# A kernel of conditioned attention: VectorE's last addition of K's first and of K's second products is made in two halves

## The chip, the cores and the metric

The kernel runs on one core of one Trainium2 chip. The metric is the device time of one execution in microseconds (us), given as the median of several runs. TensorE, VectorE, ScalarE, GpSimd and SyncE are the core's engines; in the profile's rows they are PE (its weight loads PEld), DVE, ACT, POOL and SP.

## What is computed

For each of 8 batch elements x has 512 rows of 512 numbers, and the heads are 16 of 32 numbers each. All is fp32. Cut to what matters, the reference is:

```python
Q = split_heads(x @ Wq.T + bq)          # 8 x 16 x 512 x 32; K and V likewise
tQ = split_heads(tokens @ Wq.T + bq)    # one conditioning row per batch element; tK likewise
cQ, cK = Q + tQ, K + tK
scores = einsum('bhqd,bhkd->bhqk', cQ, cK) / sqrt(32)
out = einsum('bhqk,bhkd->bhqd', softmax(scores), V)
return x + out.transpose(0, 2, 1, 3).reshape(8, 512, 512)
```

## The kernel before

**Tiling.** The heads are taken four at a time: four heads of 32 numbers fill the 128 partitions, so a batch element has G = 4 groups of heads, and there are T = 32 groups, numbered t. For a group, TensorE makes the scores with queries in the partitions (`row_scores`, L641), VectorE takes their row maxima (L593, L650), ScalarE makes exponentials of half of them with their row sums (L701). The other half is made with keys in the partitions (`exponentials_of_rest`, `joined`: L772 puts the maxima into PSUM, L785 adds the scores, L799 takes the exponential). VectorE and DMAs turn the kept half (L660, L682), and TensorE multiplies by V (L840). PSUM is one tile of 8 banks of 512 columns that the code hands out itself: `banks(i)` is the i-th bank of the current order, `released` says in which order banks come free, and the next step's scores go into them.

**Projections by seven products.** Q, K and V of the next batch element are made between these steps. For two groups at a time (u = 0 or 1) the 2 x 2 blocks of weights and x are combined so that seven products of half size do (`product`, L462; each is eight matmuls of 256 columns, four for half of it). They come in two parts. *First* makes products 1, 7, 6 and half of product 2; *other*, called second here, makes 4, 5, the other half of 2, and 3. The four results of a pair of groups are c1 (128 x 512, as two halves of 256), c2 (likewise), and c12 and c22, which are the right halves of c1 and c2. For K, c1 and c2 are the two groups' K as later scores read it.

- K's first (`first_by_others` with `mixed` None): products 1 and 7 fill one bank (`one_`), 6 and then 2 another (`two_`; 6 its right half, 2 its left). VectorE copies the first bank to c2 (L530) and sets c1 to the second bank plus the copied product 1 on both halves (L531). GpSimd then adds c12 to c22 (L533).
- K's second (`other_products` with `bias`): products 4 and 5 fill one bank, 2 and then 3 another (2 the left half, 3 the right). VectorE adds to c12 (L555), makes c2 with its bias (L557, recorded as L487 in `plus`), and adds the second bank and the bias to c1 (L560, recorded as L487).

**The order of the work** is written out by hand: `thirds(t, made)` holds, for each of the 28 groups t = 1 to 28, three steps (i = 0, 1, 2), each with scores, exponentials and one of the twelve items of the list `MADE`. One group out of two has K's first as its last item; K's second is the second item of the following group. The projections of batch elements 1 to 7 are made there, so each of the two stands 14 times. Each engine executes its own instructions in the order in which they are written. An instruction waits on semaphores of other engines, and of its own, where it needs their results or their room.

Of the kernel before, what the change touches and what calls it, by code (L numbers as in the profile page):

```python
# [12 lines left out]
ALU = mybir.AluOpType  # L13
# [4 lines left out]
def kernel(  # L18
# [38 lines left out]
    nc = tc.nc  # L57
# [58 lines left out]
    def banks(i, n=1):  # L116

        row = row_of[0] or [at_end[j] for j in TURNS[turn[0]]]
        j = row[i]
        if n == 1:  # L120
            return psum[:, j, :]
        k = row[i + 1]
        return psum[:, j : k + 1 : k - j, :]
# [273 lines left out]
    def pair_of(t, n):  # L397

        if (n, t // 2) not in pairs:
            pairs[n, t // 2] = qkp.tile([P, 2, S], F32, tag=n, name=f"{n}T_{t // 2}")  # L400
        return pairs[n, t // 2]
# [50 lines left out]
    def product(n, b, u, i, pt, kcs=(0, 1)):  # L452

        for kc in kcs:
            w = block_of_w(n, i, u, kc)
            if n == "v":
                still, moving = block_of_x(b, i, kc, slice(u * P, (u + 1) * P)), w
            else:
                still, moving = w, block_of_x(b, i, kc, slice(0, HS))
            for j in range(HG):  # L460
                r = slice(j * HD, (j + 1) * HD)
                nc.tensor.matmul(  # L462
                    pt[r], still[:, r], moving, start=(kc == kcs[0]), stop=(kc == kcs[-1])
                )

    def twice(a):
        return a.unsqueeze(1).broadcast_to([P, 2, HS])

    def halves(a):
        return a.rearrange("p (h s) -> p h s", h=2)  # L470


    def parts_of(n, b, u):

        if n == "v":
            v = vs[b % 2]
            return v[:, u::2, :HS], v[:, u + 2, :HS], v[:, u::2, HS:], v[:, u + 2, HS:]
        o = pair_of(b * G + u * 2, n)
        return halves(o[:, 0, :]), o[:, 0, HS:], halves(o[:, 1, :]), o[:, 1, HS:]

    def plus(n, b, u, g, o, pt, rest):

        if n == "v":
            nc.vector.tensor_tensor(o, pt, rest, ALU.add)
        else:
            add = tok[:, "qk".index(n), u * 2 + g, b : b + 1]
            nc.vector.scalar_tensor_tensor(o, pt, add, rest, ALU.add, ALU.add)  # L487
# [22 lines left out]
    def first_by_others(n, b, u, dens, at, last, mixed):  # L510

        one_, two_ = halves(banks(at[0])), halves(banks(at[1]))
        c1, c12, c2, c22 = parts_of(n, b, u)
        product(n, b, u, 1, one_[:, 0])
        product(n, b, u, 7, one_[:, 1])
        product(n, b, u, 6, two_[:, 1])
        product(n, b, u, 2, two_[:, 0], (0,))
        if mixed:
            dens((0, 1))
            nc.scalar.copy(c2, one_)  # L520
            dens((2, 3))
            nc.vector.tensor_tensor(c1, two_, twice(c2[:, 0, :]), ALU.add)
            last()
        else:
            dens((0, 1))
            if mixed is False:
                dens((2, 3))
            if mixed is None:
                dens((2, 3))
                nc.vector.tensor_copy(c2, one_)  # L530
                nc.vector.tensor_tensor(c1, two_, twice(c2[:, 0, :]), ALU.add)  # L531
                last()
                nc.gpsimd.tensor_tensor(c22, c22, c12, ALU.add)  # L533
                return
            else:
                nc.scalar.copy(c2, one_)
                nc.scalar.copy(c1, two_)
            last()
            nc.gpsimd.tensor_tensor(c12, c12, c2[:, 0, :], ALU.add)
            nc.gpsimd.tensor_tensor(c22, c22, c12, ALU.add)  # L540
            nc.gpsimd.tensor_tensor(c1[:, 0, :], c1[:, 0, :], c2[:, 0, :], ALU.add)
            return
        nc.gpsimd.tensor_tensor(c22, c22, c12, ALU.add)

    def other_products(n, b, u, dens, small, at, bias=False):

        dens()
        one_, two_ = banks(at[0]), banks(at[1])
        product(n, b, u, 4, one_[:, :HS])
        product(n, b, u, 5, one_[:, HS:])  # L550
        small()
        product(n, b, u, 2, two_[:, :HS], (1,))
        product(n, b, u, 3, two_[:, HS:])
        c1, c12, c2, c22 = parts_of(n, b, u)
        nc.vector.tensor_tensor(c12, one_[:, HS:], c12, ALU.add)  # L555
        if bias and n != "v":
            plus(n, b, u, 1, c2, halves(one_), twice(c22))  # L557
        else:
            nc.vector.tensor_tensor(c2, halves(one_), twice(c22), ALU.add)
        plus(n, b, u, 0, c1, halves(two_), c1)  # L560
        if n != "v":
            for g in range(2):
                qkT[n, b * G + u * 2 + g] = pair_of(b * G + u * 2, n)[:, g, :]
# [462 lines left out]
    advance()  # L1026
    row_max(0, 2)
    other_products("q", 0, 1, lambda: denominators(0, 2), nothing, (0, 1))
    advance()
    row_max(0, 3)  # L1030
# [5 lines left out]
    row_max(1, 0)  # L1036
    transpose_max(0, banks(1), nc.scalar.copy)
    other_products("k", 0, 1, lambda: denominators(1, 0), nothing, (0, 2))
    turn_x(NC + 1)
    load_blocks()  # L1040
# [44 lines left out]
    row_max(1, 2)  # L1085
    denominators(1, 2)
    other_products("v", 0, 0, nothing, nothing, (0, 2))
    turn_x(NC + 3)
    load_blocks()
# [32 lines left out]
    def products(b, n, u, product, alone, dens, last, plain):  # L1122

        if product == "first":
            first_by_others(n, b, u, dens, (4, 5) if alone else (0, 1), last, plain)
        else:
            at = (4, 5) if alone else (0, 3)
            if n == "v" and not plain:
                other_by_others(n, b, u, dens, nothing, at)
            else:  # L1130
                other_products(n, b, u, dens, nothing, at, True)
            last()
        if alone:
            released(6, 7, 0, 1, 2, 3, 4, 5)
        elif product == "first":
            released(2, 3, 4, 5, 6, 7, 0, 1)
        else:
            released(1, 2, 4, 5, 6, 7, 0, 3)
# [118 lines left out]
    def one_item(b, n, u, product, at, dens, last):  # L1257

        if n == "v" and product == "first":
            first_of_v(b, u, at)  # L1260
        elif product == "first":
            first_by_others(n, b, u, dens, at, last, False)
        elif n == "v":
            other_by_others(n, b, u, dens, nothing, at)
        else:
            other_products(n, b, u, dens, nothing, at, True)
# [182 lines left out]
    b, g = divmod(t, G)  # L1449
# [52 lines left out]
```

## Time and profile before

| what | value |
| --- | --- |
| median of 3 runs | 649.97 us (649.82 to 650.51) |
| span of the profiled execution | 648.4 us |
| time of the profiled execution by itself | not recorded apart from the three runs; their median lies 1.6 us above the span |
| mean granted TensorE clock | 0.998 |
| busy: PE, DVE, ACT, POOL | 641.6, 600.1, 533.9, 410.6 us |
| VectorE instructions | 845 |

A row of the timeline gives the start in us from the start of the span, the duration in us, engine, line, operation, tile written and tiles read, shape, how many equal instructions were merged, and in brackets how long the engine was idle before it and what ended that. A row of the groups gives count, busy time, mean ns of one, and idle time before. A row of the waits says who waited for whom: us in total, times, longest. The starts of neighbouring rows of an engine can lie closer than a duration, since an operation's end overlaps the next one's beginning. TensorE's matmul ends are modelled.

### The profile page before, as it was taken

To read this page: it belongs to the slowest core of one execution; us is meant where nothing else is said; L and a number is where in the kernel's file an instruction comes from. 1 tells how busy PE (TensorE), PEld (TensorE's weight loads), DVE (VectorE), ACT (ScalarE), POOL (GpSimd) and SP (SyncE) were. 2 spreads that over 40 slices of the span, in tenths; PEclk is the share of its full clock that TensorE was granted. 3 is DMA by queue.
4 is the path that set the end of the run, shared out by engine and by line. 5 is a ranking of instruction groups with operands and counts; after the bars stand their busy time and mean duration, and the time that the engine had idled before them with its cause. 6 is when DMAs were issued, how large, how long until landed. Compare 5 with 4: busy or idle time off the path is not lost. (4 is left out here: it accounts for less than half of the span.)

```text
span 648.4 us, 24814 instructions
## 1 busy us (share of the span) xinstructions
PE 641.6 (99%) x9856; PEld 356.7 (55%) x9856; DVE 600.1 (93%) x845; ACT 533.9 (82%) x1364; POOL 410.6 (63%) x651
## 2 busy tenths in 40 slices
PE   9999999999999999999999999999999999999997
PEld 8445555556555555555555555555555555555531
DVE  3799999999999999999999999999999999999887
ACT  2479888889888989888888988898988888898564
POOL 3633655686665776758567776558766576665650
PEclk9999999999999999999999999999999999999999
DMA  7615688878888788977888978788888767797921
GB/s 191 107 27 84 131 164 172 168 169 191 168 171 174 158 182 177 200 156 153 181 178 170 201 154 186 161 175 169 179 193 162 153 144 164 153 188 155 199 48 34
DMA packets 248457, 102.02 MB, mean 157 GB/s; under 512 B 229962, under 2 KB 230474, under 8 KB 248340
## 3 DMA queue, kind: packets, MB, share of 16 engines
q1 hardware_dynamic: 234196, 65.54, 53.6%
q0 software_dynamic: 12384, 33.83, 20.2%
q8 instruction: 78, 1.28, 0.8%
q10 hardware_dynamic: 1760, 1.05, 0.5%
q14 instruction: 39, 0.32, 0.1%
HBM read 19.75 MB, written 8.39 MB: 43 GB/s over the span
## 5 line engine op out<-in xcount | busy, mean ns | idle before, releaser
L593 DVE TENSOR_REDUCE nmax<-psum 128x1 f32<-128x512 f32 x279 | 177.5, 675 | 9.3 <-PE psum L641 4.9
L701 ACT ACTIVATE psum<-psum,nmax 128x512 f32<-128x512 f32 x248 | 165.3, 678 | 3.6 <-DVE nmax L593 3.0
L641 PE MATMUL psum<-kT,qT 32*128 32x512 f32 x1024 | 162.0, 612 | 0.0
L701 ACT ACTIVATE store<-psum,nmax 128x512 f32<-128x512 f32 x204 | 139.6, 701 | 24.9 <-DVE nmax L593 24.7
L682 POOL DMA_DIRECT2D store<-store x258 | 129.0, 504 | 48.9 <-DMA store<-store 31.8
L799 ACT ACTIVATE store<-psum 128x512 f32<-128x512 f32 x232 | 119.8, 602 | 33.2 <-PE psum L785 33.2
L660 DVE STREAM_TRANSPOSE store<-store 128x1024 f32<-128x1024 f32 x116 | 138.9, 1217 | 0.0
L650 DVE TENSOR_REDUCE nmax<-psum 128x2 f32<-128x1024 f32 x98 | 118.8, 1212 | 0.0
L840 PE MATMUL psum<-store,v 128*32 128x256 f32 x1856 | 106.8, 381 | 0.9 <-DMA store<-store 0.9
L840 PEld LDWEIGHTS psum<-store,v 128*32 128x32 f32 x1856 | 57.2, 110 | 57.9 <-ACT wT_q L632 21.2
L913 POOL TENSOR_TENSOR res<-res,recs 128x512 f32<-128x512 f32 x30 | 31.4, 1046 | 89.0 <-DVE res L912 89.0
L785 PE MATMUL psum<-qT,kT 32*128 32x256 f32 x928 | 83.8, 374 | 0.0
L641 PEld LDWEIGHTS psum<-kT,qT 32*128 32x128 f32 x1024 | 61.5, 183 | 35.4 <-issue 17.8
L785 PEld LDWEIGHTS psum<-qT,kT 32*128 32x128 f32 x928 | 60.8, 184 | 5.9 <-issue 0.3
L701 ACT ACTIVATION_READ_ACCUMULATOR psum<-psum,nmax 128x1 f32 x248 | 55.0, 222 | 0.0
L203 POOL TENSOR_TENSOR xr<-xr,bvs 128x512 f32<-128x512 f32 x30 | 38.6, 1285 | 16.4 <-DMA xr<-in_x_dram 15.7
L462 PE MATMUL psum<-wc_v,xc 128*32 128x256 f32 x768 | 47.7, 379 | 0.0
L462 PE MATMUL psum<-xc,wc_q 128*32 128x256 f32 x720 | 44.7, 379 | 0.0
L462 PE MATMUL psum<-xc,wc_k 128*32 128x256 f32 x720 | 44.5, 379 | 0.0
L701 ACT ACTIVATION_READ_ACCUMULATOR store<-psum,nmax 128x1 f32 x204 | 44.3, 217 | 0.0
L914 POOL TENSOR_TENSOR res<-res,xr 128x512 f32<-128x512 f32 x30 | 38.3, 1278 | 2.3
L462 PE MATMUL psum<-xT,wT_k 128*32 128x256 f32 x480 | 34.5, 382 | 0.0
(191 smaller groups left out, 972.4 us busy)
## 6 DMA issues: line engine op xcount, KB each, us to landing
store<-store SPq DMA_DIRECT2D x264, 128.0 KB, 2.7
store<-store POOLq DMA_DIRECT2D x258, 128.0 KB, 3.8
out_dram<-res SPq DMA_DIRECT2D x122, 64.0 KB, 3.7
xr<-in_x_dram SPq DMA_DIRECT2D x120, 64.0 KB, 4.2
x<-in_x_dram SPq DMA_DIRECT2D x112, 64.0 KB, 3.3
w_q<-in_L_cond_Wq_dram SPq DMA_DIRECT2D x4, 256.0 KB, 3.9
w_v<-in_L_cond_Wv_dram SPq DMA_DIRECT2D x16, 64.0 KB, 2.5
w_k<-in_L_cond_Wk_dram SPq DMA_DIRECT2D x16, 48.0 KB, 2.7
```

Source lines behind the costliest of these rows:

```text
L203: nc.gpsimd.tensor_tensor(xr[t], xr[t], bias, ALU.add)
L462: nc.tensor.matmul(pt[r], still[:, r], moving, start=(kc == kcs[0]), stop=(kc == kcs[-1]))
L593: nc.vector.tensor_reduce(nmax[t][:, qc, j : j + 1, 0], pt, AX.X, ALU.max, negate=True)
L641: nc.tensor.matmul(pt, qkT["q", t][r, qc * P : (qc + 1) * P], qkT["k", t][r, :], start=True, stop=True,)
L650: nc.vector.tensor_reduce(nmax[t][:, qc, pr * 2 : pr * 2 + 2, 0], pt, AX.X, ALU.max, negate=True)
L660: nc.vector.transpose(e, e)
L682: (nc.gpsimd if here else nc.sync).dma_start(to, of)
L701: nc.scalar.activation(to, of, AF.Exp, bias=nmax[t][:, qc, j, :], accum_out=sums[t][:, qc, j, :],)
L785: nc.tensor.matmul(banks(j)[:, i * HS : (i + 1) * HS], qkT["k", t][r, kc * P : (kc + 1) * P], qkT["q", t][r, KQ * P :], start=False, stop= ...
L799: nc.scalar.activation(e[:, j], banks(j), AF.Exp)
L840: nc.tensor.matmul(pt[j * HD : (j + 1) * HD, half * HS : (half + 1) * HS], vs[b % 2][:, kc, (g * HG + j) * HD : (g * HG + j + 1) * HD], e, ...
L914: nc.gpsimd.tensor_tensor(y, y, xr.pop(t), ALU.add)
```

## The change

Both additions that end in c1, at L531 (K's first) and at L560 (K's second), are written as two additions of 256 columns each. In K's first the right half (i = 1, product 6) comes first, in K's second the left half (i = 0, product 2), which is the order in which TensorE issues the products of that bank. Nothing else is changed; line numbers behind L531 move by one, behind L560 by five.

```diff
             if mixed is None:
                 dens((2, 3))
                 nc.vector.tensor_copy(c2, one_)
-                nc.vector.tensor_tensor(c1, two_, twice(c2[:, 0, :]), ALU.add)
+                for i in (1, 0):
+                    nc.vector.tensor_tensor(c1[:, i, :], two_[:, i], c2[:, 0, :], ALU.add)
                 last()
                 nc.gpsimd.tensor_tensor(c22, c22, c12, ALU.add)
                 return
...
-        plus(n, b, u, 0, c1, halves(two_), c1)
+        if bias and n == "k":
+            for i in range(2):
+                plus(n, b, u, 0, c1[:, i, :], halves(two_)[:, i], c1[:, i, :])
+        else:
+            plus(n, b, u, 0, c1, halves(two_), c1)
```

What stands in VectorE's queue at K's first of batch element 1, u = 0, before. The names are those of the built program: kT_1022 is the K of a pair of groups, nmax a group's maxima, and the brackets hold the engines whose semaphores the instruction waits for (PE_49 is TensorE, DVE_49 VectorE itself):

```order
L593 TENSOR_REDUCE nmax_1013<-psum 128x1 [waits PE_49] x2
L650 TENSOR_REDUCE nmax_1013<-psum 128x2 [waits PE_49]
L530 COPY kT_1022<-psum 128x512 [waits PE_49,Activation_49]
L531 TENSOR_TENSOR kT_1022<-psum,kT_1022 128x512 [waits DVE_49,PE_49,Activation_49]
L660 STREAM_TRANSPOSE store<-store 128x4x256
L593 TENSOR_REDUCE nmax_1013<-psum 128x1 [waits PE_49] x3
```

The same place of VectorE's queue in the changed program:

```order
L598 TENSOR_REDUCE nmax_1013<-psum 128x1 [waits PE_49] x2
L655 TENSOR_REDUCE nmax_1013<-psum 128x2 [waits PE_49]
L530 COPY kT_1022<-psum 128x512 [waits PE_49,Activation_49]
L532 TENSOR_TENSOR kT_1022<-psum,kT_1022 128x256 [waits DVE_49,PE_49,Activation_49]
L532 TENSOR_TENSOR kT_1022<-psum,kT_1022 128x256
L665 STREAM_TRANSPOSE store<-store 128x4x256
L598 TENSOR_REDUCE nmax_1013<-psum 128x1 [waits PE_49] x3
```

The one addition became two; the first has all the waits, the second, which reads product 2, has none. K's second of the same pair in VectorE's queue, before:

```order
L650 TENSOR_REDUCE nmax_1013<-psum 128x2 [waits PE_49]
L555 TENSOR_TENSOR kT_1022<-psum,kT_1022 128x256 [waits PE_49,Activation_49,Pool_49]
L487 SCALAR_TENSOR_TENSOR kT_1022<-psum,tok,kT_1022 128x512
L487 SCALAR_TENSOR_TENSOR kT_1022<-psum,tok,kT_1022 128x512 [waits DVE_49,PE_49,Activation_49]
L660 STREAM_TRANSPOSE store<-store 128x4x256
L593 TENSOR_REDUCE nmax_1273<-psum 128x1 [waits PE_49] x2
```

And in the changed program:

```order
L655 TENSOR_REDUCE nmax_1013<-psum 128x2 [waits PE_49]
L556 TENSOR_TENSOR kT_1022<-psum,kT_1022 128x256 [waits PE_49,Activation_49,Pool_49]
L487 SCALAR_TENSOR_TENSOR kT_1022<-psum,tok,kT_1022 128x512 [waits DVE_49]
L487 SCALAR_TENSOR_TENSOR kT_1022<-psum,tok,kT_1022 128x256 [waits PE_49,Activation_49]
L487 SCALAR_TENSOR_TENSOR kT_1022<-psum,tok,kT_1022 128x256 [waits DVE_49]
L665 STREAM_TRANSPOSE store<-store 128x4x256
L598 TENSOR_REDUCE nmax_1275<-psum 128x1 [waits PE_49] x2
```

Here too the wait for TensorE stands at the first half; the second half, which reads product 3, waits for VectorE's own earlier addition to c12. TensorE's queue behind K's second, before; the scores (L641) read this K:

```order
L772 LDWEIGHTS onesb
L772 MATMUL psum<-maxT_957,onesb 128x512 [waits Activation_49]
L785 MATMUL psum<-qT_363,kT_454 128x256 x8
L641 MATMUL psum<-kT_1022,qT_889 128x512 [waits DVE_49,Activation_49]
L641 MATMUL psum<-kT_1022,qT_889 128x512
L641 MATMUL psum<-kT_1022,qT_889 128x512 [waits Activation_49]
L641 MATMUL psum<-kT_1022,qT_889 128x512
L462 MATMUL psum<-wT_v,xc 32x256 [waits Activation_49]
```

TensorE's rows are the same after the change but for their line numbers; the scores then wait for the second half. ScalarE's, GpSimd's and SyncE's rows are the same as well.

## The prediction, made before the changed kernel ran

> **What bounds the kernel now.** I read the page first, for the shares of the engines, then the groups by form for the price of each operation, then the timelines of VectorE, TensorE and the weight loads at one K second and one K first, and last the waits.
>
> ```profile
> PE 641.6 (99%) x9856; PEld 356.7 (55%) x9856; DVE 600.1 (93%) x845; ACT 533.9 (82%) x1364; POOL 410.6 (63%) x651
> ```
>
> TensorE and VectorE are both near full, and neither the 99% nor the 93% says which of them waits for the other. TensorE's rows tell least: the ends of its matmuls are modelled, so its waits show as longer blocks and as idle time of the weight loads (PEld), not as idle time of PE. So I go to the two places of the change. First K's second products, the batch element whose addition starts at 175.41 us; VectorE, TensorE, the weight loads:
>
> ```profile
> 174.16 0.42 DVE L555 TENSOR_TENSOR kT<-psum,kT 128x256 f32<-128x256 f32 x1 [0.18 <-ACT psum L701]
> 174.50 0.74 DVE L487 SCALAR_TENSOR_TENSOR kT<-psum,tok,kT 128x512 f32<-128x512 f32 x1
> 175.41 0.75 DVE L487 SCALAR_TENSOR_TENSOR kT<-psum,tok,kT 128x512 f32<-128x512 f32 x1 [0.17 <-PE psum L462]
> 176.08 1.23 DVE L660 STREAM_TRANSPOSE store<-store 128x1024 f32<-128x1024 f32 x1
> 177.44 1.29 DVE L593 TENSOR_REDUCE nmax<-psum 128x1 f32<-128x512 f32 x2
> ...
> 175.45 1.03 PE L785 MATMUL psum<-qT,kT 32*128 32x256 f32 x16
> 176.31 1.14 PE L641 MATMUL psum<-kT,qT 32*128 32x512 f32 x8
> 177.38 1.07 PE L462 MATMUL psum<-wT_v,xc 128*32 128x256 f32 x16
> ...
> 176.28 0.34 PEld L641 LDWEIGHTS psum<-kT,qT 32*128 32x128 f32 x8 [0.20 <-ACT psum L701]
> ...
> 175.88 0.25 ACT L701 ACTIVATION_READ_ACCUMULATOR psum<-psum,nmax 128x1 f32 x1
> ```
>
> VectorE's last addition (the second L487) waits 0.17 us for TensorE's last product and ends at 175.41 + 0.75 = 176.16. The next scores (L641) read the K that it has just written, and their weight load starts 0.12 us later, at 176.28. The row puts that wait down to ScalarE; but ScalarE's last exponential, with its read-out, had ended at 175.88 + 0.25 = 176.13, so VectorE is the later one. Behind the scores VectorE itself stands idle from 176.08 + 1.23 = 177.31 to 177.44, until they are there. So here the path runs TensorE, this addition, TensorE, VectorE. What the late weights cost TensorE shows beside the same block after q's second products, where the weights were there in time:
>
> ```profile
> 157.65 1.03 PE L641 MATMUL psum<-kT,qT 32*128 32x512 f32 x8
> 158.60 1.07 PE L462 MATMUL psum<-xT,wT_k 128*32 128x256 f32 x16
> ```
>
> There the block takes 158.60 - 157.65 = 0.95 us to the next product, behind K's second 177.38 - 176.31 = 1.07: TensorE already loses 0.12 us here. Now K's first products, the addition at 161.96 us:
>
> ```profile
> 161.04 0.68 DVE L530 COPY kT<-psum 128x512 f32<-128x512 f32 x1
> 161.96 0.69 DVE L531 TENSOR_TENSOR kT<-psum,kT 128x512 f32<-128x512 f32 x1 [0.24 <-ACT store L701]
> 162.56 1.23 DVE L660 STREAM_TRANSPOSE store<-store 128x1024 f32<-128x1024 f32 x1
> ...
> 161.22 0.61 PE L462 MATMUL psum<-xT,wT_k 128*32 128x256 f32 x8
> 161.76 2.07 PE L641 MATMUL psum<-kT,qT 32*128 32x512 f32 x16
> 163.76 2.58 PE L840 MATMUL psum<-store,v 128*32 128x256 f32 x44
> ...
> 162.70 0.30 PEld L641 LDWEIGHTS psum<-kT,qT 32*128 32x128 f32 x7 [0.22 <-DVE kT L531]
> ...
> 164.41 0.69 ACT L701 ACTIVATE store<-psum,nmax 128x512 f32<-128x512 f32 x1 [0.90 <-DVE nmax L593]
> ```
>
> The addition ends at 162.65, and a weight load of the scores, which go into the bank that it read, starts at 162.70: this wait, too, ends at the addition. The block of sixteen lasts 163.76 - 161.76 = 2.00 us to L840; behind V's second products the same sixteen take 1.93:
>
> ```profile
> 104.41 2.00 PE L641 MATMUL psum<-kT,qT 32*128 32x512 f32 x16
> 106.34 3.66 PE L840 MATMUL psum<-store,v 128*32 128x256 f32 x64
> ```
>
> ScalarE cannot take up a delay behind it either: at 164.41 it has waited 0.90 us for VectorE's maxima, which stand behind the addition in VectorE's queue. The waits of the whole run say that these are no single cases:
>
> ```profile
> PEld psum L641 <- DVE kT L531: 2.4, 11, 0.2
> DVE kT L531 <- ACT store L701: 3.4, 14, 0.3
> DVE kT L487 <- PE psum L462: 2.4, 14, 0.2
> ```
>
> **The change part by part.** *What it moves.* It is meant to let VectorE read the half that TensorE finished first while the other half is being made. The rows of the program order (in the section on the change) say that it does not: of the two halves only the first waits for TensorE, and the second, which reads the product that TensorE finishes last, waits for none. Both can be safe only if the first half's wait already stands for the last product. So the first half starts when the whole addition starts now, the 0.17 and 0.24 us of idle time stay, and nothing is removed. TensorE's, ScalarE's, GpSimd's and SyncE's rows are the same before and after. GpSimd's L533 reads only the half written first and may start some 0.3 us sooner; its sum is needed only by K's second, whose first addition (L555) stands at 174.16, some 11 us behind the addition at 162.65, so I count that at nothing; if that cover were gone, it would be a gain of 0.3 us at each. The new waits of VectorE on its own queue are for results at least one operation back that have ended by then: nothing.
>
> On the first half's wait the Trainium skill has a rule, in "PSUM — Partial Sum Buffer", section "PSUM bank collisions raise a hardware error": guard PSUM by bank and quadrant and not by address, since another engine's access to another address of the same bank still collides. Each pair of halves shares one bank, so by that rule the first half has to wait for both products, and the time is the sum below; without it, it is the first rival. The order's rows agree; no timed run here shows it yet.
>
> *What it adds.* Fourteen times (seven batch elements by two halves of the heads) one more VectorE instruction at each of the two places. The price is the distance from start to start, since the end of one operation overlaps the next:
>
> ```profile
> L531 DVE TENSOR_TENSOR kT<-psum,kT 128x512 f32<-128x512 f32 x14 | 9.7, 692 | 3.4 <-ACT store L701 3.4
> L555 DVE TENSOR_TENSOR kT<-psum,kT 128x256 f32<-128x256 f32 x15 | 6.3, 423 | 2.5 <-ACT psum L701 2.3
> L487 DVE SCALAR_TENSOR_TENSOR kT<-psum,tok,kT 128x512 f32<-128x512 f32 x29 | 21.5, 746 | 2.4 <-PE psum L462 2.4
> L487 DVE SCALAR_TENSOR_TENSOR kT<-psum,tok,kT 128x256 f32<-128x256 f32 x1 | 0.5, 483 | 0.1
> ...
> 40.53 0.48 DVE L487 SCALAR_TENSOR_TENSOR kT<-psum,tok,kT 128x256 f32<-128x256 f32 x1
> 40.93 0.70 DVE L372 STREAM_TRANSPOSE xT<-x 128x512 f32<-128x512 f32 x1
> ```
>
> - K's first: a plain addition of 256 columns holds VectorE 174.50 - 174.16 = 0.34 us, two of them 0.68; the one of 512 holds it 162.56 - 161.96 = 0.60. So +0.08 us, fourteen times 1.1 us.
> - K's second: the addition with bias of 256 columns holds it 40.93 - 40.53 = 0.40 us, two of them 0.80; the one of 512 holds it 176.08 - 175.41 = 0.67. So +0.13 us, fourteen times 1.8 us.
>
> The bounds: the trace has no such pair back to back. Below, the second instruction is free if something hides it; a gain is excluded as long as the first half cannot start sooner. Above, with no overlap the durations count: 2 x 0.423 - 0.692 = 0.15 and 2 x 0.483 - 0.746 = 0.22, together 14 x 0.37 = 5.2 us. I take the start-to-start values, since every VectorE row quoted overlaps its successor by about 0.08 us.
>
> The Trainium skill's "Perfetto Trace Analysis", section "Optimizing Scalar/DVE Operations", gives about 125 ns of overhead per VectorE instruction on PSUM; by that, as an estimate, 28 more are 3.5 us, and the time would be 653.5. My rows give 0.08 and 0.13, and they decide.
>
> *What lies on the path.* Both additions end later by what they gain in length, and a TensorE weight load follows each at once (162.70, 176.28). TensorE is already late there by 2.00 - 1.93 = 0.07 and 1.07 - 0.95 = 0.12 us, so no slack is left, and I pass the whole delay on. Between the two places TensorE's blocks stand end to end, and VectorE and ScalarE wait for each other's next step, so I see nothing that gives it back. Sum: 1.1 + 1.8 = 2.9 us. The profiled span becomes 648.4 + 2.9 = 651.3; the median of the runs, 649.97, lies 1.6 us above the span, and with that the time is **652.9 us**.
>
> **The rivals.**
> - *It does what it says (faster).* If the first half waited for its own product alone, K's second could start it at 174.50 + 0.67 = 175.17, the second half at 175.17 + 0.40 = 175.57, and end at 176.05 instead of 176.16: 0.11 us sooner. K's first could start its half when the copy has ended, 161.04 + 0.68 = 161.72, with some 0.04 to the start, and the second 0.34 later at 162.10, ending at 162.52 instead of 162.65: 0.13 sooner. Fourteen times 0.24 is 3.4 us: 646.6. It decides from the point where the idle time before the halves falls under 0.1 us. For it speaks that idle time; against it the single wait in the order's rows. 0.03.
> - *The delay is hidden (same).* Behind q's second, where the weights are in time, an L785 block takes 0.86 us to the scores:
>
> ```profile
> 80.11 1.03 PE L785 MATMUL psum<-qT,kT 32*128 32x256 f32 x16
> 80.97 1.04 PE L641 MATMUL psum<-kT,qT 32*128 32x512 f32 x8
> ...
> 165.50 0.66 DVE L637 TENSOR_REDUCE nmax<-wT_q 128x1 f32<-128x512 f32 x1
> ```
>
>   Behind K's second the scores start at 176.31, which is 175.45 + 0.86, so their first matmul is not late, and VectorE has 0.13 us to spare before 177.44. If the weights may come later still without moving the matmuls, all is covered: 650.0. Against it: the two blocks that are already longer. 0.10.
> - *Only K's second counts (slower).* At K's first the scores held back belong to the second set, which VectorE reads only behind L637 at 165.50, 2.8 us after the weight load; if TensorE makes up those 0.08 us, 1.8 us remain: 651.8. 0.17.
> - *Two halves do not overlap (slower).* 5.2 us: 655.2. 0.06.
>
> **How the numbers follow.** My forecast, both terms on the path, has 0.64. A measurement of this kernel tells about 0.2% (1.3 us) from no change. Slower by more than that: 0.64 + 0.17 + 0.06 = 0.87; within it: 0.10; faster: 0.03. The range 650.8 to 654.0 holds the forecast and the case of K's second alone, 0.81; the hidden case, the faster one and the one without overlap lie outside.
>
> **What would show it.** The idle time before each first half should stay near 0.24 and 0.17 us; the halves should stand 0.34 and 0.40 us from start to start; VectorE's busy time should grow by up to 5.2 us (the durations count there); the weight load behind K's first should wait longer for VectorE than its 2.4 us in all; the blocks behind both should not shrink; the span should be near 651.3. I am wrong in the first step if the idle time before the first halves is gone, and in the last if the additions end later but the next scores' products start at the same distance from L785 as now.

## The result and the profile after

The changed kernel takes **652.42 us** (median of 6 runs, 652.00 to 653.15), the kernel before, timed beside it, 650.25 us (6 runs, 649.82 to 650.83): a ratio of 1.0031, 95% interval 1.0021 to 1.0042. A second timing gave 653.06 against 650.24 us, 1.0039 (1.0026 to 1.0052). So the kernel is slower by 2.2 and 2.8 us, where 2.9 was predicted. The profiled execution of after has a span of 650.2 us at a granted clock of 0.999; before's was 648.4.

The engines' busy times of after, from the page:

```profile
PE 644.1 (99%) x9856; PEld 358.2 (55%) x9856; DVE 601.7 (93%) x873; ACT 533.6 (82%) x1364; POOL 409.8 (63%) x651
```

VectorE has 28 instructions more, and 1.6 us more of busy time, in which overlapping instructions count once. K's first in the timeline of after (VectorE; TensorE; its weight loads):

```profile
161.34 0.68 DVE L530 COPY kT<-psum 128x512 f32<-128x512 f32 x1
162.26 0.76 DVE L532 TENSOR_TENSOR kT<-psum,kT 128x256 f32<-128x256 f32 x2 [0.24 <-ACT store L706]
162.93 1.24 DVE L665 STREAM_TRANSPOSE store<-store 128x1024 f32<-128x1024 f32 x1
...
162.07 2.14 PE L646 MATMUL psum<-kT,qT 32*128 32x512 f32 x16
...
164.13 3.23 PE L845 MATMUL psum<-store,v 128*32 128x256 f32 x56
...
163.03 0.34 PEld L646 LDWEIGHTS psum<-kT,qT 32*128 32x128 f32 x7 [0.24 <-issue]
```

The two halves are one row (x2). The idle time before them is still 0.24 us. From their start to the transposition's it is now 162.93 - 162.26 = 0.67 us instead of 0.60, and the scores' block takes 164.13 - 162.07 = 2.06 us instead of 2.00. K's second of the same pair:

```profile
174.87 0.74 DVE L487 SCALAR_TENSOR_TENSOR kT<-psum,tok,kT 128x512 f32<-128x512 f32 x1
175.80 0.88 DVE L487 SCALAR_TENSOR_TENSOR kT<-psum,tok,kT 128x256 f32<-128x256 f32 x2 [0.18 <-PE psum L462]
176.59 1.24 DVE L665 STREAM_TRANSPOSE store<-store 128x1024 f32<-128x1024 f32 x1
...
177.95 1.29 DVE L598 TENSOR_REDUCE nmax<-psum 128x1 f32<-128x512 f32 x2
...
174.61 1.05 PE L462 MATMUL psum<-xT,wc_k 128*32 128x256 f32 x16
175.59 0.40 PE L777 MATMUL psum<-maxT,onesb 3*128 3x512 bf16 x4
175.82 1.03 PE L790 MATMUL psum<-qT,kT 32*128 32x256 f32 x16
176.82 1.14 PE L646 MATMUL psum<-kT,qT 32*128 32x512 f32 x8
177.89 1.07 PE L462 MATMUL psum<-wT_v,xc 128*32 128x256 f32 x16
```

Idle before the halves: 0.18 us, 0.01 more than before. They hold VectorE 176.59 - 175.80 = 0.79 us instead of 0.67. The scores (L646) start 1.00 us behind L790 instead of 0.86, and the next product follows 1.07 us behind them, as it did before: TensorE is later by the whole 0.14 us. Over the run, from the waits and the groups:

```profile
DVE kT L532 <- ACT store L706: 3.4, 14, 0.3
DVE kT L487 <- PE psum L462: 2.4, 13, 0.2
```

```profile
L487 DVE SCALAR_TENSOR_TENSOR kT<-psum,tok,kT 128x256 f32<-128x256 f32 x29 | 12.8, 480 | 2.9 <-PE psum L462 2.2 <-PE psum L777 0.5
L532 DVE TENSOR_TENSOR kT<-psum,kT 128x256 f32<-128x256 f32 x28 | 10.6, 420 | 3.4 <-ACT store L706 3.4
```

The two waits that the change was made for are the same 3.4 and 2.4 us as before, but for one: at 291.59 us the wait at K's second is 0.53 us long, once, and the row of the groups counts it under L777.

**How late it is along the way.** To see where time is lost, take the start of the same instruction in both profiles, early and late: the transposition of x (L372) that stands at 75.65 us in before, and TensorE's last scores (L1305, in after L1310) ahead of the last groups' products with V (L840, L845). Before:

```profile
75.65 0.67 DVE L372 STREAM_TRANSPOSE xT<-x 128x512 f32<-128x512 f32 x1
...
617.01 0.59 PE L1305 MATMUL psum<-qT,kT 32*128 32x512 f32 x2
618.53 1.93 PE L840 MATMUL psum<-store,v 128*32 128x256 f32 x32 [0.93 <-DMA store<-store]
```

After:

```profile
75.65 0.67 DVE L372 STREAM_TRANSPOSE xT<-x 128x512 f32<-128x512 f32 x1
...
619.86 0.59 PE L1310 MATMUL psum<-qT,kT 32*128 32x512 f32 x2
620.38 1.93 PE L845 MATMUL psum<-store,v 128*32 128x256 f32 x32
```

Equal at 75.65 us, 2.85 us late at 617.01. Then before waits 0.93 us for a DMA that brings the last turned exponentials, and after does not wait: the products with V start only 1.85 us late, and the span is 1.8 us longer. So the profile of after shows 2.85 us lost by the end of the fourteen pairs, and 1.0 us given back in one wait at the end.

### The profile page after: what moved, and what is told of

Same layout as the page of the kernel before. It is cut to its first block, busy times and chain, and to the rows that moved or that the text cites. A ratio compares the mean times of both kernels' runs of the same rounds, so it can differ in the third digit from the quotient of the medians.

```text
span 650.2 us, 24842 instructions
## 1 busy us (share of the span) xinstructions
PE 644.1 (99%) x9856; PEld 358.2 (55%) x9856; DVE 601.7 (93%) x873; ACT 533.6 (82%) x1364; POOL 409.8 (63%) x651
## 5 line engine op out<-in xcount | busy, mean ns | idle before, releaser
L646 PE MATMUL psum<-kT,qT 32*128 32x512 f32 x1024 | 162.7, 613 | 0.3 <-DVE kT L487 0.3
L845 PE MATMUL psum<-store,v 128*32 128x256 f32 x1856 | 106.8, 381 | 0.0
L845 PEld LDWEIGHTS psum<-store,v 128*32 128x32 f32 x1856 | 57.1, 110 | 57.0 <-ACT wT_q L637 21.2
L790 PE MATMUL psum<-qT,kT 32*128 32x256 f32 x928 | 83.8, 374 | 0.0
L646 PEld LDWEIGHTS psum<-kT,qT 32*128 32x128 f32 x1024 | 62.8, 184 | 37.0 <-issue 20.5
L790 PEld LDWEIGHTS psum<-qT,kT 32*128 32x128 f32 x928 | 60.9, 184 | 5.6 <-issue 0.3
```

Source lines behind the costliest of these rows:

```text
L646: nc.tensor.matmul(pt, qkT["q", t][r, qc * P : (qc + 1) * P], qkT["k", t][r, :], start=True, stop=True,)
L790: nc.tensor.matmul(banks(j)[:, i * HS : (i + 1) * HS], qkT["k", t][r, kc * P : (kc + 1) * P], qkT["q", t][r, KQ * P :], start=False, stop= ...
L845: nc.tensor.matmul(pt[j * HD : (j + 1) * HD, half * HS : (half + 1) * HS], vs[b % 2][:, kc, (g * HG + j) * HD : (g * HG + j + 1) * HD], e, ...
```

## The experiments

Every kernel here computes the whole reference. The edits are shown against the changed kernel, except where said. TensorE and VectorE signal the end of their work by semaphore events; the traces keep the times of these, and where a row leaves open who ended a wait they are used below. "Lost" in the table is how much later than before the last scores ahead of that wait start, less how much later L372 starts (this takes out different beginnings of up to 0.8 us); "end wait" is the idle time of TensorE before the products with V behind these scores. Rows of five kernels name ScalarE as what ended the end wait, but in each of the eleven profiles that have one the products start 0.19 to 0.20 us behind a landing on the same DMA queue.

| kernel | us, before beside it | ratio (95%) | lost, us | end wait, us |
| --- | --- | --- | --- | --- |
| before | 650.25 | 1 | 0 | 0.93 |
| after | 652.42, 650.25 | 1.0031 (1.0021 to 1.0042) | 2.85 | 0 |
| after again | 653.06, 650.24 | 1.0039 (1.0026 to 1.0052) | 2.84 | 0.81 |
| K's first alone | 650.85, 650.06 | 1.0008 (0.9999 to 1.0017) | 0.61 | 0.95 |
| K's second alone | 651.93, 650.06 | 1.0027 (1.0018 to 1.0036) | 1.68 | 0.82 |
| halves in reverse order | 653.38, 650.06 | 1.0046 (1.0034 to 1.0059) | 2.65 | 1.17 |
| quarters | 657.85, 650.06 | 1.0118 (1.0104 to 1.0132) | 7.82 | 0.41 |
| a bank for each half | 651.85, 650.14 | 1.0028 (1.0017 to 1.0039) | 1.63 | 1.00 |
| bias by GpSimd, no halves | 648.92, 650.14 | 0.9983 (0.9974 to 0.9992) | -0.77 | 0.34 |
| the same again | 649.15, 650.06 | 0.9983 (0.9974 to 0.9992) | -0.74 | 0.99 |
| bias by GpSimd, halves | 652.72, 650.24 | 1.0041 (1.0029 to 1.0054) | 1.18 | 2.85 |
| the same again | 651.80, 650.06 | 1.0024 (1.0015 to 1.0033) | 1.41 | 2.08 |

The theory: a pair of halves starts no sooner than the whole addition, and costs one more instruction's fixed part, which TensorE takes over in full. The rivals: the delay is hidden at one place or at both; the order of the halves matters; the loss has nothing to do with the fixed part.

### K's first alone

```diff
-        if bias and n == "k":
-            for i in range(2):
-                plus(n, b, u, 0, c1[:, i, :], halves(two_)[:, i], c1[:, i, :])
-        else:
-            plus(n, b, u, 0, c1, halves(two_), c1)
+        plus(n, b, u, 0, c1, halves(two_), c1)
```

> Only K's first addition is in two halves; K's second is one addition as before. Theory A (length on the path: the halves start when the whole one did, each extra instruction delays VectorE and TensorE by its own length, and up to 1.0 us of the total is taken up at the end where TensorE waited 0.93 us for a DMA): by the end of the last K second, near 597 us of the span, the steps stand 14 x 0.065 = 0.9 us later than before; the time is 0 to 0.9 us above before. Theory B (the cost comes from K's second alone, K's first is hidden behind scores that VectorE reads later): no shift at 597 us and no change of the time. Theory C (no cover at the end): shift 0.9 and time +0.9 us.

Measured: 0.8 us more in the median, with an interval that just takes in no change. The profile decides here: comparing the starts of the same VectorE instructions, they fall back by 0.062 us at nearly every K's first and by nothing at nearly every K's second, in all 14 x 0.062 = 0.87 us. (Such steps are good to about 0.003 us, by which neighbouring rows one takes.) The table's 0.61 is that, less 0.26 us gained once near 295 us, where before has a wait of 0.46 us that is shorter in all kernels with halves. So K's first counts, and apart from such single places nothing gives it back.

### K's second alone

```diff
-                for i in (1, 0):
-                    nc.vector.tensor_tensor(c1[:, i, :], two_[:, i], c2[:, 0, :], ALU.add)
+                nc.vector.tensor_tensor(c1, two_, twice(c2[:, 0, :]), ALU.add)
```

> Only K's second addition is in two halves. Theory A: shift near 597 us of 14 x 0.137 = 1.9 us, time 0.9 to 1.9 us above before. Theory B: the whole of the measured difference, shift 2.8 us and time +2.2 us. Theory C: shift 1.9 and time +1.9 us.

Measured: 1.9 us more; 0.137 us at each K's second, nothing at the K's firsts, 14 x 0.137 = 1.92 us. Less the same 0.26 us this is the 1.68 of the table. The two kernels' steps together make 14 x (0.062 + 0.137) = 2.8 us, and the changed kernel lost 2.85. Its steps are the same two, so the edits add; in its total the 0.26 us and 0.09 us gained near 99 us are cancelled by the 0.35 us more of the one long wait at 291.59 us, whose cause is open.

### The halves in reverse order

```diff
-                for i in (1, 0):
+                for i in (0, 1):
...
-            for i in range(2):
+            for i in (1, 0):
```

> Both additions in halves, each pair in the opposite order (the half that TensorE finishes last is taken first). Theory A (the first half waits for the whole bank whatever its product): the same as the changed kernel, shift 2.8 us near 597 us, time within 0.5 us of it, idle time before the first halves 0.24 and 0.17 us again. Rival (the order in which TensorE finishes matters, part of the halves' work is done sooner): slower than the changed kernel by up to 14 x 0.24 = 3.4 us, with longer idle time before the halves.

Now the half that TensorE finishes last is read first. The step at K's first is the same, 0.063 us; at K's second it is 0.125, 0.014 less than with the change's order. K's first and K's second in its timeline, VectorE:

```profile
162.69 0.76 DVE L532 TENSOR_TENSOR kT<-psum,kT 128x256 f32<-128x256 f32 x2 [0.24 <-ACT store L706]
...
175.31 0.74 DVE L487 SCALAR_TENSOR_TENSOR kT<-psum,tok,kT 128x512 f32<-128x512 f32 x1
176.22 0.88 DVE L487 SCALAR_TENSOR_TENSOR kT<-psum,tok,kT 128x256 f32<-128x256 f32 x2 [0.17 <-PE psum L462]
177.01 1.23 DVE L665 STREAM_TRANSPOSE store<-store 128x1024 f32<-128x1024 f32 x1
```

The waits of 0.24 and 0.17 us and the 177.01 - 176.22 = 0.79 us are those of the changed kernel, but for 0.01 us of the wait. If a half waited for its own product alone, the half finished first would wait less. The 0.014 us are no work of the halves: with the change's order the first half at K's second starts 0.093 us behind TensorE's signal; in reverse order it is 0.079 us, and 0.080 for the whole addition in before. In 14 places that is 0.2 us, the difference of the two kernels in the table. Why the signal is taken up later there is open. The time itself is 1.0 us above the first timing of after, more than the 0.5 I expected, and 0.3 above the second, with overlapping intervals; its end wait is 1.17 us against 0 in after's first profile. That spread of the end wait was not in my expectation.

### Quarters

```diff
-                    nc.vector.tensor_tensor(c1[:, i, :], two_[:, i], c2[:, 0, :], ALU.add)
+                    for f in (slice(0, P), slice(P, HS)):
+                        nc.vector.tensor_tensor(c1[:, i, f], two_[:, i, f], c2[:, 0, f], ALU.add)
...
-                plus(n, b, u, 0, c1[:, i, :], halves(two_)[:, i], c1[:, i, :])
+                for f in (slice(0, P), slice(P, HS)):
+                    plus(n, b, u, 0, c1[:, i, f], halves(two_)[:, i, f], c1[:, i, f])
```

> Each of the two additions in four quarters of 128 columns, in the order of the changed kernel. By the start-to-start times a quarter holds VectorE about 0.21 us at K's first and 0.27 us at K's second. Theory A: 4 x 0.21 - 0.60 = 0.24 and 4 x 0.27 - 0.67 = 0.40 us more than before at each place, shift near 597 us 14 x 0.64 = 9.0 us, time 8.0 to 9.0 us above before. Rival (only the first extra instruction costs, the rest hide): time within 1 us of the changed kernel.

Measured: 7.8 us more, a little under the 8.0 to 9.0 expected; 0.19 us at each K's first and 0.39 at each K's second, 14 x 0.58 = 8.1 us. With three instructions more instead of one this is 0.063 and 0.13 apiece, about the values of the halves. So the price goes by the number of instructions; my 0.08 us for the plain addition was too high here as well.

### A bank for each half

Product 3 goes into a bank of its own, in K's second alone, and the order in which banks come free is adapted. K's first is one addition again, as before; the lines below do not show that:

```diff
+        own = bias and n == "k"
+        three = banks(2) if own else two_
...
-        product(n, b, u, 3, two_[:, HS:])
+        product(n, b, u, 3, three[:, HS:])
...
-                plus(n, b, u, 0, c1[:, i, :], halves(two_)[:, i], c1[:, i, :])
+                plus(n, b, u, 0, c1[:, i, :], halves((two_, three)[i])[:, i], c1[:, i, :])
...
+                if n == "k":
+                    released(1, 4, 5, 6, 7, 2, 0, 3)
```

> As before, but product 3 of K's second goes into a bank of its own, and c1 is added in two halves, each behind its own product; K's first as before. The next step takes its banks in another order for that, so that TensorE's fourth bank there comes free with ScalarE's third exponential instead of an earlier one. Theory A (halves in one bank wait for the whole bank): here the first half starts while TensorE still makes product 3, 0.2 to 0.4 us sooner than before, and the addition ends about 0.1 to 0.3 us sooner behind product 3; what the other order of the banks costs TensorE, up to 0.3 us at each of 14 places, comes on top: time from 3 us below to 3 us above before. Rival (halves never start sooner, whatever the bank): the first half starts behind product 3 as before, and the time is at least 1.9 us above before.

In the program order each half now has a TensorE wait of its own. The same place in its timeline, VectorE and TensorE:

```profile
175.03 0.42 DVE L557 TENSOR_TENSOR kT<-psum,kT 128x256 f32<-128x256 f32 x1 [0.18 <-ACT psum L707]
175.37 1.53 DVE L487 SCALAR_TENSOR_TENSOR kT<-psum,tok,kT 128x512 f32<-128x512 f32 x3
176.81 1.24 DVE L666 STREAM_TRANSPOSE store<-store 128x1024 f32<-128x1024 f32 x1
...
175.12 1.05 PE L462 MATMUL psum<-xT,wc_k 128*32 128x256 f32 x16
176.09 0.65 PE L778 MATMUL psum<-maxT,onesb 3*128 3x512 bf16 x4
176.38 1.23 PE L791 MATMUL psum<-qT,kT 32*128 32x256 f32 x16
177.35 1.12 PE L647 MATMUL psum<-kT,qT 32*128 32x512 f32 x8
178.40 0.42 PE L462 MATMUL psum<-wT_v,xc 128*32 128x256 f32 x4
```

The three additions (c2 and both halves of c1, one row) run without a gap: the wait of 0.18 us is gone. In 13 of the 14 places the first half starts 0.17 to 0.18 us ahead of TensorE's signal for product 3 (here at 176.03, the signal at 176.21); the other, at 99.53 us, starts behind it. In after it starts 0.09 us or more behind that signal in all 14. From the start of the last products to the transposition it is 176.81 - 175.12 = 1.69 us, in after 176.59 - 174.61 = 1.98, and in before 176.08 - 174.24 = 1.84, where 174.24 is this row:

```profile
174.24 1.05 PE L462 MATMUL psum<-xT,wc_k 128*32 128x256 f32 x16
```

So with a bank for each half the change does what it was meant to do: VectorE has the K 0.29 us sooner than with one bank, 0.15 sooner than before. TensorE has nothing of it: from L778 to the next product it needs 178.40 - 176.09 = 2.31 us, as in after (177.89 - 175.59 = 2.30; in before it is 2.16), and VectorE waits more often for scores elsewhere. Its row in the waits; in after it is 4.9 us, 10 times:

```profile
DVE nmax L599 <- PE psum L647: 9.1, 22, 2.1
```

The kernel stays 1.7 us above before. Which part of the new order of banks costs this was not separated.

### The bias by GpSimd, without halves

Both halves are undone. GpSimd, which is idle over a third of the time, adds the bias to c1 behind K's first; VectorE's last addition in K's second becomes a plain one. Against before:

```diff
                 nc.gpsimd.tensor_tensor(c22, c22, c12, ALU.add)
+                add = tok[:, 1, u * 2, b : b + 1].unsqueeze(2).broadcast_to([P, 2, HS])
+                nc.gpsimd.tensor_tensor(c1, c1, add, ALU.add)
...
-        plus(n, b, u, 0, c1, halves(two_), c1)
+        if bias and n == "k":
+            nc.vector.tensor_tensor(c1, halves(two_), c1, ALU.add)
+        else:
+            plus(n, b, u, 0, c1, halves(two_), c1)
```

> As before, but GpSimd adds K's bias to c1 behind its own addition at K's first, and K's second adds c1 without the bias, as one plain addition of 512 columns. Theory A (the length of this addition is on the path, both ways): it holds VectorE 0.60 instead of 0.67 us and ends 0.06 us sooner, the shift near 597 us is 14 x -0.06 = -0.8 us, the time 0 to 0.8 us below before. Rival (the path is full only for delays, TensorE gives nothing back when the addition is shorter): no shift. If GpSimd's extra 14 operations disturb VectorE or the DMAs that GpSimd issues, the shift is above zero.

K's second in its timeline, VectorE and TensorE:

```profile
175.34 0.69 DVE L563 TENSOR_TENSOR kT<-psum,kT 128x512 f32<-128x512 f32 x1 [0.17 <-PE psum L462]
175.95 1.24 DVE L665 STREAM_TRANSPOSE store<-store 128x1024 f32<-128x1024 f32 x1
...
176.25 1.08 PE L646 MATMUL psum<-kT,qT 32*128 32x512 f32 x8
177.25 1.07 PE L462 MATMUL psum<-wT_v,xc 128*32 128x256 f32 x16
```

The addition holds VectorE 0.61 us instead of 0.67, and the scores' block shrinks from 1.07 to 1.00. At each K's second the kernel gains 0.057 us, 14 x 0.057 = 0.8 us. This is the same path walked the other way: what the last addition gains in length, the run gains. At 648.92 us it is the fastest kernel here, by more than the 0.8 us expected. To see how much of its 1.2 us was the end wait, it was timed again:

> The kernel with K's second bias added by GpSimd, timed a second time. Theory (the shorter addition on the path is worth 0.06 us at each K second, the rest of the first timing's 1.2 us was the wait for the last DMAs at about 616 us, which varies between executions): between 0.2 and 1.3 us below the kernel before (ratio 0.998 to 0.9997); VectorE's steps at 597 us again 0.6 to 0.9 us earlier than before's. Rival (the whole gain is chance): within 0.3 us of the kernel before, and the steps not earlier.

649.15 against 650.06, and again 0.74 us gained on the way, with an end wait of 0.99 us, so about as long as before's. The gain of 0.9 us then is nearly the gain on the way; the rest of the first 1.2 fits the short end wait of its profile, 0.34 us.

### The bias by GpSimd, with halves, and after again

The same kernel, with both plain additions to c1 in halves as in the change. Beside it the changed kernel was timed once more:

> The changed kernel once more, since its steps stood 2.8 us later than before near 597 us and its median was only 2.2 us above. Theory A with a chance at the end (TensorE waits there 0 to 1.2 us for the last DMAs of the turned exponentials, differently in every execution): steps again 0.062 us later at each K first and 0.137 us at each K second; time 2.2 to 3.3 us above before. Rival (the end gives back 1.0 us each time, whenever the steps before come later): time at most 2.2 us above before.

> The kernel in which GpSimd adds K's bias, with the change on top: both plain additions in two halves. Theory A (what a split costs is the fixed part of the operation that is repeated): plain halves cost 0.065 us at both places, so 14 x 0.13 = 1.8 us above the kernel with GpSimd's bias and 14 x (0.065 + 0.007) = 1.0 us above before. Rival (a split costs 0.137 us at K's second because of that place, whatever the operation): 14 x 0.20 = 2.8 us above the kernel with GpSimd's bias, 2.0 us above before.

After again lost 2.84 us on the way (after: 2.85), had an end wait of 0.81 us, and came out 2.8 us above before: so the 1.0 us given back in the first profile was no effect of the change.

With GpSimd's bias, the halves lost 1.18 - (-0.77) = 1.95 us on the way. That is 14 x 0.062 for K's first and 14 x 0.077 for K's second: a plain addition in halves costs 0.06 to 0.08 us, the one with bias 0.137. At K's second both hold the 0.014 us by which the first half takes up TensorE's signal later; without it they are 0.063 and about 0.125 us. But the time is 2.5 us above before, more than either expectation said. In the profile the end wait is 2.85 us, and the clock falls behind it. Two rows, and the windows of the two stretches (the columns behind the engines are granted clock, DMA share, GB/s):

```profile
618.12 0.59 PE L1312 MATMUL psum<-qT,kT 32*128 32x512 f32 x2
621.56 3.05 PE L847 MATMUL psum<-store,v 128*32 128x256 f32 x32 [2.85 <-DMA store<-store]
```

```profile
618.00:622.00 4.00, 1.15 (x17) 0.35 (x13) 2.44 (x4) 1.87 (x4) 3.20 (x4) 1.00 0.55 106
622.00:626.00 4.00, 4.00 (x46) 2.79 (x42) 0.87 (x2) 0.45 (x2) 0.84 (x1) 0.57 0.38 66
```

To tell chance from a property of this kernel it was timed again:

> The same with both plain additions in halves, timed a second time. Theory (halves cost 0.062 and about 0.07 us at the two places, 14 times each, also as plain additions; the first timing's further 1.5 us came from the wait for the last DMAs at 618 us, 2.85 us long in its profile, a chance): steps at 597 us 1.6 to 2.1 us later than those of the kernel with GpSimd's bias, and the time 1.5 to 2.2 us above it, so 0.5 to 1.7 us above the kernel before. Rival (something in this kernel makes its last DMAs late every time): steps the same, but the wait at about 618 us again over 2 us and the time 2.2 us or more above the kernel before.

1.7 us above before, 1.41 us lost on the way, and an end wait of 2.08 us. Of the 1.41, 1.15 us were lost by the last K's second, as in the first profile (1.17); that is 1.9 us behind the kernel with GpSimd's bias, as the theory said. The rest comes in one place at 613 us. The time just misses the theory's range, 1.74 us above before instead of at most 1.7 and 2.65 above the kernel with GpSimd's bias instead of at most 2.2, but stays under the rival's 2.2 us above before; the wait fits the rival. Both profiles of this kernel have an end wait of over 2 us, and none of the ten profiles of the others has more than 1.17, so its last DMAs may well land late more often; why is open.

## Why the prediction was right

- **The halves start no sooner: right.** The idle time before them is 0.24 and 0.18 us (predicted 0.24 and 0.17), 3.4 and 2.4 us in all. Reversing the halves leaves it; at K's second, giving each its own bank removes it. So there the first half waits for the last product because the two share a bank. At K's first the row names ScalarE, which the prediction passed over, but TensorE ends that wait too: in all 14 places of before and of after VectorE's wait instruction passes 0.03 to 0.04 us behind TensorE's signal of the last product, and the addition starts 0.04 to 0.05 us after it. That the bank is the reason there as well was not tested with a bank for each half. The rule of the Trainium skill that was weighed ("PSUM — Partial Sum Buffer", "PSUM bank collisions raise a hardware error": guard by bank and quadrant, not by address) agrees with the waits: 0.18 us with one bank, none with two. Whether a read of the one half during the write of the other would harm the chip was not tried.
- **The price: right for K's second, somewhat high for K's first.** Predicted 0.13, measured 0.137 us (1.9 us in all, predicted 1.8). Of this some 0.125 is the second instruction and 0.014 the later start, which the prediction did not have. Predicted 0.08, measured 0.062 (0.9 us, predicted 1.1). The sum is 2.8 us instead of 2.9; that it comes so near is in part luck, since the two errors have opposite signs. Start to start was the right measure; by the durations it would have been 5.2. The page "Perfetto Trace Analysis", section "Optimizing Scalar/DVE Operations", of the Trainium skill gives about 125 ns of overhead per VectorE instruction on PSUM; that agrees with the addition with bias (125 ns in reverse order, 137 in the change's) and is twice the 62 ns of the plain one.
- **The whole delay reaches TensorE: right.** Behind K's first the scores' block became 0.06 us longer. Behind K's second it kept its 1.07 us but starts 0.14 us later behind L790, so there it is the first scores that are now late, not the block that grows. The experiments with one of the two additions in halves put the terms apart: 14 x 0.062 and 14 x 0.137 us. The rivals that hid the delay, at both places or at K's first, are refuted by the 0.062 us that remain at K's first.
- **"I see nothing that gives it back": not quite.** It holds up to 617 us, but for the single places near 99, 291 and 295 us, which cancel in after. Behind that, the wait of TensorE for the last turned exponentials, which the prediction did not look at, lay between 0 and 1.17 us in ten of the twelve profiles, and in one kernel at 2.08 and 2.85. In after's first profile it was 0, and 1.0 of 2.85 us came back; in after again it was 0.81. The median of 652.42 (0.5 us under the forecast) and the second one of 653.06 (0.2 us above) lie on both sides of 652.9; how near a single timing comes is partly chance.
- **One sign showed only under another name.** The wait of the weight load behind K's first for VectorE was to grow from 2.4 us. No row by that name is left in after; instead this one grew, from 17.8 us and 54 times:

```profile
PEld psum L646 <- issue: 20.5, 65, 0.4
```

  Its 11 more cases are as many as the vanished row had, and its 2.7 us more are a little above that row's 2.4. The semaphore events show that it is the same wait: at all 14 places, in before and in after, the weight load that waits for VectorE starts 0.04 us behind VectorE's signal at the end of the addition (in the place shown 163.07 behind 163.03, as one of the loads merged into the row at 163.03; in before 162.70 behind 162.66).

## What to carry to other kernels

Before an operation is split so that its first part can start earlier, see what that part would wait for: where both parts read one bank, and the program guards by the bank, only the fixed part of one more instruction is bought, here 0.06 us for a plain addition and 0.13 to 0.14 for one with bias. Where such an operation was the last link ahead of a full engine, its length from start to start counted one to one in both directions: a bias moved to an idle engine gave 0.06 us per step, and 0.17% of the median in both timings. A shift that grows in equal steps along the run says more than a total, which one chance wait at the end moved by a third of the effect.

## What the runs showed of the hardware

- One more VectorE instruction in a split cost 0.062 us for an addition of two tensors (128 x 256, PSUM and SBUF), and 0.125 us (halves in reverse order) to 0.137 us (the change's order) for the form with a bias per partition, with the same number of elements in all.
- The last wait for DMAs varied from 0 to 0.81 us between two profiles of the changed kernel, from 0.34 to 0.99 between two of the kernel with GpSimd's bias, and from 0 to 1.17 over ten profiles, so the profile of one execution bears an uncertainty of about 1 us at its end alone.
- After 2.85 us without matmuls TensorE's granted clock stood at 0.57 in the window from 622 to 626 us, and 32 matmuls took 3.05 instead of 1.93 us; after 2.08 us idle, in the second profile of the same kernel, they took 1.93:

```profile
621.45 1.93 PE L847 MATMUL psum<-store,v 128*32 128x256 f32 x32 [2.08 <-DMA store<-store]
```
